# Layer 0 of a four-layer image network on one Trainium2 core: another way to build the position biases, the softmax denominators and the order of the score tiles

## The chip, the core and the metric

One core of one Trainium2 chip runs the whole network in a single launch. The time of a run is the device time in microseconds (us) of that core. A measurement is the median of three runs; a profile is one further execution that the hardware profiler recorded.

The engines are named as the profile names them: PE is the matrix engine, PEld its weight loads, DVE the vector engine, ACT the scalar engine, POOL the GpSimd engine, SP the engine that here only issues DMAs. An entry such as SPq or POOLq is the instruction queue of that engine.

## The reference, cut to what matters

The input `x` is 2 images of 64 by 64 positions with 128 channels. Four layers follow one another; only layer 0 is changed. It adds to `x` a self-attention over the 4096 positions of each image, 4 heads of 32 dimensions, with a bias that depends on the relative row and the relative column of the two positions:

```
qkv = einsum('bhwc,cd->bhwd', _gn(x), w_qkv);  q, k, v = split(qkv)      # _gn: group normalization
rw[q, k] = q . pos_emb_w[column(k) - column(q) + 63]
rh[q, k] = q . pos_emb_h[row(k) - row(q) + 63]
scores = einsum('bnqd,bnkd->bnqk', q, k) / sqrt(32) + rw + rh
attn = softmax(scores, axis=-1)
x = x + einsum('bnqk,bnkd->bnqd', attn, v)
```

(The two bias lines are the reference's `relative_position_bias` with its padding and reshaping written out as an index.) The other layers, a triangle product, two attentions and two expert stages, come after it and are the same in both kernels.

## The kernel before, in words

`layer0` (line 273) works in four **units**, one for each image b and pair of heads p. For a unit it needs the rows of q and k, and for each query the biases against the 64 rows and the 64 columns. Scores with biases are made by one matmul with a contraction of 64: 32 rows of k, then 32 rows that hold a one-hot pattern (in `ka`, lines 300 to 319), against 32 rows of q, 16 rows of row biases and 16 rows of column biases (in `mv`). The one-hot rows pick the two biases that belong to a key.

**Preparation of a unit.** `tokens(b)` (line 333) transposes the image by PE into `xT`, takes its statistics and normalizes it in one DVE instruction (line 353). `project(b)` (line 356) makes v, k (`pk`, line 384) and q (`pq`, line 390) from it; k and q go to DRAM scratch `kd` and `qd` by SP DMAs and q also back into `xT`. `biases(b, p)` (line 400) makes the biases with small matmuls: for each of 64 columns one [64 x 128] by [64 x 64] product with a shifted window of a table `tab` (line 411), and the same for each of 64 rows (line 426). Eight of them fill a PSUM bank, ACT copies it out (lines 419 and 434), and SP writes it to the DRAM scratch `wd` (line 421, one DMA) and `hd` (line 435, eight DMAs). These products have the right diagonal already, because each of the 64 takes its own window of the table.

**Main loop** (line 574). A unit has 8 blocks of 512 queries (`qb`), a block has 4 steps over key rows (`xb`), a step has 8 score tiles (4 `yb` times 2 `s`). A score tile `sc` is [128 keys x 2 heads x 512 queries], made by 4 matmuls that use the four 64 x 64 quarters of the array (line 598). ACT takes the exponential into an `es` tile (line 612; ring of 8), DVE adds it to `acc` (line 620), and PE multiplies it by v into `o` (line 552, four column groups of 32). The order on PE is written out: four score tiles, then the `o` products of four tiles that are two pairs behind (`while len(waiting) > 2`), then one **piece** of side work. A piece is one step of a generator in `side`: the preparation of the next unit, cut at its `yield`s. The first tile of a block is written by ACT into `acc` itself and added to in place.

`mv` has two copies; `prefill(at + 2)` (line 622) queues on SP the loads of the step after next. SP thus carries these loads and all scratch writes, in order.

**Block end.** `finish` (line 502) copies `o` out, and on PE makes 4 products with `fold` (line 513) and 8 products of a [128 x 128] piece of `acc` with a column of ones (line 518), which give the denominators per query. DVE then copies, inverts, multiplies and adds to `x` (lines 527 to 539).

Before the main loop, preparation of unit 0 runs alone (lines 475 to 483). POOL and DVE each build one of the two one-hot tables at the very start (line 305).

Of the kernel before, what the change touches and what calls it, by code (L numbers as in the profile page):

```python
# [38 lines left out]
class Net:  # L39
# [56 lines left out]
    def rstd_parts(self, out, var, eps, n):  # L96

        nc = self.nc
        v = self.small.tile([P, n], F32, tag=f"rs_v{n}", name="rs_v")
        nc.vector.tensor_scalar(v, var, eps, None, ALU.add)  # L100
        s = self.small.tile([P, n], F32, tag=f"rs_s{n}", name="rs_s")
        nc.scalar.activation(s, v, AF.Sqrt)
        yield
        r = self.small.tile([P, n], F32, tag=f"rs_r{n}", name="rs_r")
        nc.vector.reciprocal(r, s)
        q = self.small.tile([P, n], F32, tag=f"rs_q{n}", name="rs_q")
        nc.vector.scalar_tensor_tensor(q, r, -0.5, r, ALU.mult, ALU.mult)
        nc.vector.tensor_tensor(q, q, v, ALU.mult)
        nc.vector.scalar_tensor_tensor(out, q, 1.5, r, ALU.add, ALU.mult)

    def group_stats(self, ps, b, xT=None):
# [3 lines left out]
        st = self.small.tile([P, NC // 4, 6], F32, tag="gst", name=f"gst{b}")  # L115
# [145 lines left out]
    def l0_tables(self, ps, pool, raw, tab):  # L261

        nc = self.nc
        nc.vector.memset(tab, 0.0)
        for i, n in enumerate("hw"):
            pt = ps.tile([P, 512], F32, tag="misc", name=f"l0pe{n}")
            nc.tensor.transpose(pt[:HD, :P], raw[:, i, :], self.ident)
            for h in range(NH):
                nc.scalar.copy(
                    tab[h * HD : (h + 1) * HD, i, : 2 * S - 1, h % 2], pt[:HD, : 2 * S - 1]  # L270
                )

    def layer0(self):
# [4 lines left out]
        pairs = 2  # L278
        with ExitStack() as st:
            wp = st.enter_context(tc.tile_pool(name="l0w", bufs=1))  # L280
            ap = st.enter_context(tc.tile_pool(name="l0b", bufs=2))
            dp = st.enter_context(
                tc.tile_pool(name="l0d", bufs=1, space=bass.MemoryType.DRAM)
            )
            w = self.load(wp, "wqkv", [P, 3 * C], ins["L0_conv_w_qkv"])
            raw = wp.tile([P, 2, HD], F32, tag="raw", name="l0raw")
            nc.vector.memset(raw, 0.0)
            for i, n in enumerate("hw"):
                nc.sync.dma_start(out=raw[: 2 * S - 1, i, :], in_=ins[f"L0_conv_pos_emb_{n}"])
            tab = wp.tile([P, 2, P, 2], F32, tag="tab", name="l0tab")  # L290
            ones = wp.tile([P, 1], F32, tag="ones", name="l0ones")
            nc.vector.memset(ones, 1.0)
            sums = wp.tile([P, 2 * pairs * 8, 4, 2], F32, tag="sums", name="l0sums")

# [5 lines left out]
            kas = []  # L300
            for i in range(2):
                ka = wp.tile([P, L], F32, tag=f"ka{i}", name=f"ka{i}")
                for lo in (32, 96):
                    for g in range(NX):
                        (nc.gpsimd, nc.vector)[i].tensor_tensor(
                            ka[lo : lo + 32, g * TB * S : (g + 1) * TB * S].rearrange(
                                "p (a x y) -> p a x y", x=TB, y=TB
                            ),
                            self.ident[lo : lo + 32, lo : lo + TB]
                            .unsqueeze(1)  # L310
                            .unsqueeze(3)
                            .broadcast_to([32, NX, TB, TB]),
                            self.ident[lo : lo + 32, lo + TB : lo + 32]
                            .unsqueeze(1)
                            .unsqueeze(1)
                            .broadcast_to([32, NX, TB, TB]),
                            ALU.add,
                        )
                kas.append(ka)

            qd = [dp.tile([P, L], F32, tag=f"qd{b}", name=f"l0qd{b}") for b in range(B)]
            kd = [dp.tile([P, L], F32, tag=f"kd{b}", name=f"l0kd{b}") for b in range(B)]
            units = [(b, pair) for b in range(B) for pair in range(pairs)]
            hd = {u: dp.tile([P, L], F32, tag=f"hd{u}", name=f"l0hd{u[0]}_{u[1]}") for u in units}
            wd = {u: dp.tile([P, L], F32, tag=f"wd{u}", name=f"l0wd{u[0]}_{u[1]}") for u in units}
# [6 lines left out]

            def tokens(ps, b):
# [3 lines left out]
                st = self.small.tile([P, NC // 4, 6], F32, tag="gst", name=f"gst{b}")  # L337
# [15 lines left out]
                nc.vector.tensor_scalar(xT, xT, gm, gr, ALU.subtract, ALU.mult)  # L353
                yield

            def project(ps, b):
# [8 lines left out]
                for n in range(NC // 4):  # L365
                    pv = ps.tile([P, 4, C], F32, tag="misc", name=f"l0pv{b}_{n}")
                    for i in range(4):
                        j = 4 * n + i
                        nc.tensor.matmul(
                            pv[:, i, :],  # L370
                            lhsT=xT[:, j * P : (j + 1) * P],
                            rhs=w[:, 2 * C :],
                            start=True,
                            stop=True,
                        )
                    for p in range(pairs):
                        nc.scalar.copy(
                            v[p][:, 4 * n : 4 * n + 4, :], pv[:, :, 2 * HD * p : 2 * HD * (p + 1)]
                        )
                    yield  # L380
                for g in range(L // 512):
                    part = blocks(xT, g)
                    pk = ps.tile([P, NX, P], F32, tag="misc", name=f"l0pk{b}_{g}")
                    nc.tensor.matmul(pk, lhsT=w[:, C : 2 * C], rhs=part, start=True, stop=True)
                    kst = ap.tile([P, NX, P], F32, tag="stage", name=f"l0kst{b}_{g}", bufs=3)
                    nc.scalar.activation(kst, pk, AF.Copy, scale=root)
                    nc.sync.dma_start(out=blocks(kd[b], g), in_=kst)
                    yield
                    pq = ps.tile([P, NX, P], F32, tag="misc", name=f"l0pq{b}_{g}")
                    nc.tensor.matmul(pq, lhsT=w[:, :C], rhs=part, start=True, stop=True)  # L390
                    qst = ap.tile([P, 512], F32, tag="stage", name=f"l0qst{b}_{g}", bufs=3)
                    nc.scalar.copy(
                        qst.rearrange("p (x a y) -> p a x y", a=NX, y=TB),
                        pq.rearrange("p a (x y) -> p a x y", y=TB),
                    )
                    nc.sync.dma_start(out=qd[b][:, g * 512 : (g + 1) * 512], in_=qst)
                    nc.scalar.copy(part, pq)
                    yield

            def biases(ps, b, p):  # L400

                grid = qTs[b].rearrange("p (x a r y) -> p x r a y", x=NX, a=NX, y=TB)
                flat = tab.rearrange("p n i h -> p n (i h)")
                rows = slice(2 * HD * p, 2 * HD * (p + 1))
                t = f"{b}_{p}"
# [1513 lines left out]
```

## Time and profile before

| | |
|---|---|
| median of three runs | 5018.42 us (5015.92 to 5019.35) |
| the profiled execution: its own time | 5015.46 us |
| the profiled execution: span from first to last instruction | 5013.6 us |
| mean granted PE clock | 0.907 |
| first score matmul of layer 0 | 142.5 us |
| last addition of layer 0 to `x` | 1830.3 us |
| block-to-block distance in unit 3, from one copy of `o` to the next | 46.86 us or 48.55 us; mean 47.81 us of seven |
| busy in layer 0 until 1835 us: PE | 1769 us |

The page of a profile has numbered parts: busy time by engine, the span in 40 slices, DMA queues, the chain of work that ended last, and the costliest groups of instructions by line with their mean duration and the idle time before them. Beside the page the trace answers questions: a timeline of a stretch, the windows view (busy time, granted clock and DMA share in given stretches), one line's instructions with their shortest, median and longest duration, and groups with their shapes kept apart. Fp32 matmuls appear as two records each, and four that use different parts of the array overlap, so busy time divided by records gives the spacing.

### The profile page before, as it was taken

How to read it: one execution, taken by the hardware profiler on the slowest of the kernel's cores; microseconds unless marked ns; L12 is line 12 of the kernel's file. 1: busy time of each engine (PE TensorE's matmuls, PEld its weight loads, DVE VectorE, ACT ScalarE, POOL GpSimd, SP SyncE). 2: the span in 40 equal slices, each digit the busy share in tenths (PEclk: the TensorE clock that was granted, in tenths of full speed). 3: DMA queues.
4: the chain of work that ended last, by engine and by line, in shares of the span. 5: the costliest groups of instructions: out<-in, count | busy, mean ns of one | idle time of the engine just before them, and what ended most of it. 6: DMA issues, size and time to landing. Idle time of an engine off the chain costs nothing.

```text
span 5013.6 us, 69136 instructions
## 1 busy us (share of the span) xinstructions
PE 4518.9 (90%) x28099; PEld 2029.4 (40%) x28099; DVE 2904.6 (58%) x4826; ACT 2372.4 (47%) x2781; POOL 681.6 (14%) x450
## 2 busy tenths in 40 slices
PE   7999999999999967468999999967999999999765
PEld 6433333443333325422233233326975444444432
DVE  2567867666878788745666655562042333333577
ACT  3556666565666643235777788841012222222200
POOL 1000000000000011114455455520011000000000
PEclk7899999999999988679999999975569999999889
DMA  4323333333233310000000000021400000000000
GB/s 126 67 56 53 54 68 72 73 82 66 48 62 54 55 29 1 6 19 1 1 1 1 1 1 1 1 70 67 118 19 1 0 0 0 0 0 0 5 13 22
DMA packets 132797, 164.95 MB, mean 33 GB/s; under 512 B 13904, under 2 KB 76208, under 8 KB 131568
## 3 DMA queue, kind: packets, MB, share of 16 engines
q1 hardware_dynamic: 110560, 143.25, 13.4%
q10 hardware_dynamic: 21904, 17.12, 1.2%
q8 instruction: 225, 3.69, 0.3%
q14 instruction: 108, 0.88, 0.1%
HBM read 130.97 MB, written 29.36 MB: 32 GB/s over the span
## 4 chain that ended last, share of the span: by engine, by line
PE 80%; DVE 12%; ACT 5%; issue 1%; DMA 1%; POOL 0%; SPq 0%; DVEq 0%; ACTq 0%; POOLq 0%
PE l0sc L598 18%; PE l0o L552 9%; PE scl L1683 9%; PE oTl L1700 9%; PE l2sc L1312 5%; PE l2pos L1213 4%; PE l2av L1364 4%; PE f3ex L1857 2%; PE f2po L1561 2%; PE f2ph L1535 2%; DVE l0acc L620 2%; PE l0pw L411 2%; ACT l2es L1350 2%; PE l0ph L426 1%; DVE x L1865 1%
## 5 line engine op out<-in xcount | busy, mean ns | idle before, releaser
L620 DVE TENSOR_TENSOR l0acc<-l0acc,l0es 128x1024 f32<-128x1024 f32 x988 | 1210.0, 1225 | 540.1 <-PE l0o L552 376.5
L612 ACT ACTIVATE l0es<-l0sc 128x1024 f32<-128x1024 f32 x992 | 940.3, 1031 | 387.1 <-PE l0sc L598 386.2
L598 PE MATMUL l0sc<-l0mv,ka 64*64 64x512 f32 x8192 | 993.3, 617 | 18.8 <-ACT l0es L612 16.5
L1708 DVE TENSOR_TENSOR accl<-accl,esl 128x1024 f32<-128x1024 f32 x240 | 294.1, 1225 | 540.7 <-ACT esl L1694 482.9
L1339 POOL TENSOR_TENSOR l2es<-l2es 128x1024 f32<-128x1024 f32 (+3 forms) x288 | 505.0, 1753 | 604.4 <-DVE l2es L1336 530.9
L598 PEld LDWEIGHTS l0sc<-l0mv,ka 64*64 64x64 f32 x8192 | 297.8, 136 | 624.3 <-issue 378.4
L1350 ACT ACTIVATE l2es<-l2es 128x1024 f32<-128x1024 f32 (+3 forms) x576 | 533.3, 977 | 6.9 <-POOL l2es L1343 6.7
L1694 ACT ACTIVATE esl<-scl 128x1024 f32<-128x1024 f32 x240 | 245.5, 1023 | 550.8 <-PE scl L1683 550.8
L552 PE MATMUL l0o<-l0es,l0v 128*32 128x512 f32 x3968 | 494.9, 602 | 0.0
L1683 PE MATMUL scl<-l3qT,l3kT 128*128 128x512 f32 x1024 | 484.1, 595 | 1.8 <-DVE bok_l L252 1.8
L1336 DVE TENSOR_SCALAR l2es<-l2sc 128x1024 f32<-128x1024 f32 (+3 forms) x272 | 306.5, 1127 | 296.4 <-PE l2sc L1312 293.7
L1700 PE MATMUL oTl<-esl,l3v 128*128 128x512 f32 x960 | 448.5, 592 | 0.0
L1326 ACT ACTIVATE l2es<-l2sc 128x1024 f32<-128x1024 f32 (+3 forms) x288 | 273.4, 949 | 261.5 <-PE l2sc L1312 258.4
L1312 PE MATMUL l2sc<-l2q,l2kT 32*128 32x512 f32 (+3 forms) x2304 | 339.4, 623 | 10.1 <-DVE l2es L1336 5.8
L1364 PE MATMUL l2av<-l2es,l2v 128*32 128x512 f32 (+3 forms) x2304 | 322.1, 580 | 8.6 <-ACT l2es L1350 8.5
L1213 PE MATMUL l2pos<-l2v,toe 128*32 128x512 f32 (+3 forms) x2304 | 299.9, 582 | 1.4 <-ACT l2v L1158 1.4
L1683 PEld LDWEIGHTS scl<-l3qT,l3kT 128*128 128x128 f32 x1024 | 192.7, 191 | 233.3 <-issue 218.7
L1700 PEld LDWEIGHTS oTl<-esl,l3v 128*128 128x128 f32 x960 | 182.4, 190 | 229.6 <-issue 225.8
L874 POOL TENSOR_TENSOR l1y<-l1y,l1gb 128x1024 f32<-128x1024 f32 x8 | 20.3, 2532 | 1860.6 <-DMA bo<-in_L_conv_bo_dram 1821.6
L552 PEld LDWEIGHTS l0o<-l0es,l0v 128*32 128x32 f32 x3968 | 106.9, 109 | 337.8 <-issue 337.8
L1312 PEld LDWEIGHTS l2sc<-l2q,l2kT 32*128 32x128 f32 x2304 | 100.6, 188 | 255.3 <-ACT l2es L1350 94.3
L1865 DVE SCALAR_TENSOR_TENSOR x<-f3ex,f3wt,x 128x128 f32<-128x128 f32 x512 | 160.2, 347 | 28.5 <-PE f3ex L1857 20.0
(438 smaller groups left out, 4310.8 us busy)
## 6 DMA issues: line engine op xcount, KB each, us to landing
l0mv<-l0qd SPq DMA_DIRECT2D x128, 256.0 KB, 7.6
l0mv<-l0hd SPq DMA_DIRECT2D x256, 128.0 KB, 7.5
l0mv<-l0wd SPq DMA_DIRECT2D x128, 128.0 KB, 5.6
l0wd<-l0rw SPq DMA_DIRECT2D x4, 2048.0 KB, 6.8
l0hd<-l0hst SPq DMA_DIRECT2D x32, 256.0 KB, 2.1
f2w<-in_L_ffn_weight_dram ACTq DMA_DIRECT2D x32, 256.0 KB, 11.9
f2w<-in_L_ffn_weight_dram ACTq DMA_DIRECT2D x8, 1024.0 KB, 5.1
f2w<-in_L_ffn_weight_dram SPq DMA_DIRECT2D x8, 1024.0 KB
```

The lines of the kernel that those rows point to most:

```text
L552: nc.tensor.matmul(o[0][at : at + HD, :], lhsT=v[:, 2 * j + s, HD * h : HD * (h + 1)], rhs=es[s][:, h, :], start=(j == 0), stop=(j == NX * ...
L598: nc.tensor.matmul(sc[64 * c : 64 * c + 64, h, :], lhsT=ka[rows, k0 : k0 + 64], rhs=mv[rows, yb, :], start=True, stop=True,)
L612: nc.scalar.activation(es, sc, AF.Exp)
L620: nc.vector.tensor_tensor(entry[5], entry[5], es, ALU.add)
L1213: nc.tensor.matmul(pos[c : c + 32, j0:, :], lhsT=toe[:, d * P + c : d * P + c + 32], rhs=v[:, n0 + j0 - d : n0 + 4 - d, :], start=(d == n0 ...
L1312: nc.tensor.matmul(sc[:, h2, off:], lhsT=kT[hs, cols], rhs=q[hs, off:], start=True, stop=True,)
L1336: nc.vector.tensor_scalar(es[:, :, lo:], sc[:, :, lo:], root, None, ALU.mult)
L1339: nc.gpsimd.tensor_tensor(part, part, part, ALU.mult)
L1350: nc.scalar.activation(e[:, :, off:], e[:, :, off:], AF.Silu)
L1364: nc.tensor.matmul(avs[i][hs, off:], lhsT=vs[b][:, k, hs], rhs=es[h // 2][:, h % 2, off:], start=(k == 0), stop=last,)
L1683: nc.tensor.matmul(sc[:, i, :], lhsT=kT[:, k * P : (k + 1) * P], rhs=qs, start=True, stop=True,)
L1700: nc.tensor.matmul(oT, lhsT=v[:, k, :], rhs=es[:, i, :], start=(k == 0), stop=(k == NC - 1),)
```

## The change

All of it is in layer 0 and its helpers.

1. **Full-width bias products.** `slope` multiplies all 127 rows of the (flipped) position table, as a [32 x 128] weight for one head, by 512 queries at once, two heads into one [128 x 2 x 512] PSUM tile. This holds the products of every query with every relative offset. It is copied out as one [128 x 1024] tile in the `es` ring and written to new DRAM scratch (`slopes`). The right diagonal is then picked by the addresses of a DMA: `skewed` reads with a row step of L and a step of L + S from one group to the next, in runs of 64 numbers. For the row biases the DMA goes from scratch to `hd`; for the column biases into a tile `tw`, which POOL copies, reordered, into `rw`; four DMAs write `rw` to `wd`. The row order in `hd` and `wd` is reversed, and the one-hot tables and the `mv` indices follow that.
2. **Queues.** Every DMA of `project` and `biases` is issued by POOL, no longer by SP. The table loads are issued by ACT, each row four times over (one copy for each head).
3. **One-hot tables on POOL.** Both are built there from a small reversed identity, after the tokens of image 0.
4. **Denominators.** `block_end` multiplies a [128 x 32] tile of ones by `acc` in four column groups, 512 queries wide, so that `zb` has the layout of `o`. ACT copies it out (with a running sum for the range check), DVE inverts 128 x 512 numbers and multiplies `os`, and the `fold` products come last; DVE adds their PSUM result to `x` directly.
5. **Rounds of eight.** A step makes its 8 score tiles, then its 16 pairs of `o` products; there is no `waiting` list. `acc` has its own tile, written first as `es[0,0] + es[0,1]`. The `es` ring is 9. One piece of side work per step, two in the last step of a block and in all steps of unit 1.
6. Small things: `tokens` normalizes in 4 parts, `project` goes by 4 groups of rows, for unit 0 some copies go to DVE, small tiles have fewer buffers.

The order in which the compiled kernel's instructions stand on the engines follows the program: on PE eight score tiles, eight tiles' `o` products, a slope. On POOL stand, ahead of the first DMA of `project`, all 16 one-hot instructions; then for each unit 32 writes of slopes, 16 skewed reads into `tw` with 8 copies between them, 16 skewed scratch-to-scratch copies into `hd` and 4 writes of `wd`.

The diff, cut to its core:

```diff
+            def skewed(t, first, rows, n):
+                at = t[:, :]
+                return bass.AP(
+                    tensor=at.tensor,
+                    offset=at.offset + first * (L + S),
+                    ap=[[L, rows], [L + S, n], [1, S]],
+                )
...
-                    nc.sync.dma_start(out=blocks(kd[b], g), in_=kst)
+                        nc.gpsimd.dma_start(out=blocks(kd[b], g), in_=kst)
...
+            def slope(ps, u, n, g, tag):
+                pt = ps.tile([P, 2, 512], F32, tag="sc", name=f"l0p{t}", bufs=tag[1])
+                for h in range(2):
+                    rows = slice((2 * p + h) * HD, (2 * p + h + 1) * HD)
...
+                    nc.tensor.matmul(
+                        pt[:, h, :],
+                        lhsT=pos[rows, "hw".index(n), :],
+                        rhs=rhs,
...
+                ev = ap.tile([P, 2, 512], F32, tag=tag[0], name=f"l0e{t}", bufs=tag[2])
...
+                for h in range(2):
+                    nc.gpsimd.dma_start(
+                        out=slopes[h, n][u][:, g * 512 : (g + 1) * 512], in_=ev[:, h, :]
+                    )
+            def biases(ps, u, tag):
...
+                def turned(g):
+                    tw = ap.tile([P, 8, S], F32, tag="tw", name=f"l0tw{b}_{p}_{g}", bufs=1)
+                    for h in range(2):
+                        nc.gpsimd.dma_start(
+                            out=tw[S * h : S * h + S],
+                            in_=skewed(slopes[h, "w"][u], 8 * g, S, 8),
+                        )
+                    nc.gpsimd.tensor_copy(
+                        rw.rearrange("p (x y) -> p y x", y=S)[:, 8 * g : 8 * g + 8, :], tw
+                    )
+                for g in range(8):
+                    slope(ps, u, "w", g, tag)
+                    if g >= 2:
+                        turned(g - 2)
+                    yield
+                for g in range(8):
+                    slope(ps, u, "h", g, tag)
...
+                    for h in range(2):
+                        nc.gpsimd.dma_start(
+                            out=hd[u][S * h : S * h + S, g * 512 : (g + 1) * 512].rearrange(
+                                "k (x y) -> k x y", y=S
+                            ),
+                            in_=skewed(slopes[h, "h"][u], 8 * g, S, 8),
+                        )
+                    yield
...
+                zb = ps.tile([P, 512], F32, tag="misc", name=f"l0zb{t}")
+                for s in range(2):
+                    for h in range(2):
+                        at = 64 * s + HD * h
+                        nc.tensor.matmul(
+                            zb[at : at + HD, :],
+                            lhsT=ones,
+                            rhs=acc[:, h, :],
...
+                r = ap.tile([P, 512], F32, tag="zs", name=f"l0zs{t}", bufs=1)
+                nc.scalar.activation(r, zb, AF.Copy, accum_out=sums[:, 0, n : n + 1])
+                yield
+                nc.vector.reciprocal(r, r)
+                nc.vector.tensor_tensor(os, os, r, ALU.mult)
...
+                if i == 1 or xb == 3:
                     piece()
+                piece()
                 prefill(at + 2)
```

## The prediction, as put on record

> **What bounds the kernel now.** I read the page's chain of waits first, then its groups, the windows view for the start, and the timeline of a steady stretch. The change touches only layer 0, the first 1830 us of a span of 5013.6 us (the execution took 5015.46 us, 3 us under the median of 5018.42).
>
> ```profile
> PE 80%; DVE 12%; ACT 5%; issue 1%; DMA 1%; POOL 0%; SPq 0%; DVEq 0%; ACTq 0%; POOLq 0%
> L620 DVE TENSOR_TENSOR l0acc<-l0acc,l0es 128x1024 f32<-128x1024 f32 x988 | 1210.0, 1225 | 540.1 <-PE l0o L552 376.5
> L598 PE MATMUL l0sc<-l0mv,ka 64*64 64x512 f32 x8192 | 993.3, 617 | 18.8 <-ACT l0es L612 16.5
> ```
>
> PE carries 80% of the chain, and the score matmuls were held for 18.8 us in all. DVE waits 540 us, so it is not the bound; but 376 of these are one wait per block: the first addition into `acc` waits until PE has read that tile as a value operand, and DVE then runs behind.
>
> ```profile
> 1512.85 3.66 PE L598 MATMUL l0sc<-l0mv,ka 64*64 64x512 f32 x32
> ...
> 1514.01 3.77 ACT L612 ACTIVATE l0es<-l0sc 128x1024 f32<-128x1024 f32 x4 [1.79 <-PE l0sc L598]
> ...
> 1516.45 1.92 PE L552 MATMUL l0o<-l0es,l0v 128*32 128x512 f32 x16
> ...
> 1518.30 3.66 PE L598 MATMUL l0sc<-l0mv,ka 64*64 64x512 f32 x32
> ```
>
> That is one PE cycle, four score tiles and four tiles' values: 5.45 us from 1512.85 to 1518.30. It holds 12 groups of four overlapping records. In the same timeline the weight loads of a group start every 0.43 us, so the work is 12 x 0.43 = 5.16 and the two switches cost 0.29. ACT needs 0.94 per tile against 1.36 of PE.
>
> ```profile
> 36.00:66.00 30.00, 22.39 (x97) 0.90 0.52 160
> 66.00:93.00 27.00, 27.00 (x127) 0.50 0.22 57
> 93.00:121.00 28.00, 27.75 (x131) 0.50 0.39 150
> 121.00:142.00 21.00, 16.08 (x71) 0.50 0.39 75
> ```
>
> This is the start (length, PE busy, records, granted clock, DMA share, GB/s). From 66 to 121 us PE does nothing but the narrow bias products of unit 0, at a granted clock of 0.50: 0.21 us a record, against 0.127 later (6.09 us for 48 records). The first score matmul comes at 142.5.
>
> **The main loop, 142.5 to 1830 us.** A clean block takes 46.86 us (from one copy of `o` to the next in unit 3); every other one takes 48.55, because PE runs a cycle at half speed (5.36 us instead of 3.66, roughly every 50 to 100 us). The mean is 47.81. I keep these 0.95 us per block.
>
> - *Rounds of eight:* 24 groups x 0.43 = 10.32, and one pair of switches, 0.29, instead of two. 10.61 a round, 42.4 a block, against 43.6: -1.2.
> - *Denominators:* the block end takes 2.9 us of PE now (24 records from 1502.94 to 1505.71 and a switch). It gets 4 `zb` products that overlap on four column groups like the values, 2 x 0.43 = 0.86, and 8 `fold` records at 2.77/24 = 0.115, 0.92, each with a switch of 0.1: 2.0 in all, -0.9.
> - *Own `acc` tile:* the remaining 0.3 us of a clean block is a hold of the score matmuls behind ACT, where DVE has not freed `es`. It goes, as DVE no longer waits 7 us per block.
>
> PE then needs 44.5 + 0.95 = 45.4 us a block. **DVE is next:** back to back, 19 additions took 25.14 us, 1.32 each, so 31 cost 40.9. New is an inversion of 128 x 512:
>
> ```profile
> L529 DVE RECIPROCAL l0ri<-l0sums 128x8 f32<-128x8 f32 x32 | 6.3, 195 | 0.0
> L1829 DVE RECIPROCAL f3ri<-f3ri 128x64 f32<-128x64 f32 x1 | 0.6, 550 | 0.0
> ```
>
> 355 ns for 56 more columns is 6.3 ns a column, so 3.4 us for 512 (an estimate from these two rows). With the product (0.69, the row of 128x512) and the addition to `x` (0.42) DVE has 45.7 us a block. That is PE's time within 1%: where no side work runs, about half of the blocks, I take 46.0. So 32 blocks cost 16 x 45.4 + 16 x 46.0 = 1462 instead of 32 x 47.81 = 1530: **-68**.
>
> - *Bias products of units 1 to 3:* lines 411 and 426 keep PE busy for 92 us after 142. Instead there are 48 slopes. Their two heads lie on different rows of the array; if they overlap, a slope is 2 x 0.43 and a switch, 0.96, if not 1.82; 46 or 87 us. The products of line 1312, also 32 rows deep, overlap (339.4 us for 2304 records, 0.147 each), so I take 46: **-46**. The first score tiles of before also came at a clock of 0.66, and pieces are fewer but larger, fewer switches: **-15**.
>
> Together the loop gains about 130 us, if nothing new holds it.
>
> **The new queue.** POOL has no DMA in the trace of before; after the change it issues, for each unit, 32 slope writes, 32 skewed copies and 4 writes of `wd`, and does 8 copies of 128x512 (1.26 us by line 968). Call the cost of one issue t. From below SP's own issues bound it: 0.34 us for `hd`, 0.38 for `kd` with four times the runs. From above I take POOL's nearest compute row:
>
> ```profile
> L305 POOL TENSOR_TENSOR ka<-ident x8: 1913/2852/2910, 1.4 to 18.5; 32x1024 f32<-32x1024 f32 x8
> L305 DVE TENSOR_TENSOR ka<-ident x8: 1214/2897/2949, 5.3 to 23.5; 32x1024 f32<-32x1024 f32 x8
> ```
>
> up to 2.9 us (1.9 while DVE is not beside it). I choose t = 1.0, nearer to SP's rows, since these are the same operation. A landing takes 2.1 to 2.3 us (writes to scratch).
>
> *Start:* 16 one-hot instructions at 1.91 keep POOL until 33 us; DVE, freed of its eight, no longer delays the statistics (they start at 24.8 now, when DVE is done), so tokens are ready by then. `project` waits for 16 issues and 4 copies and some landings: 33 + 16t + 5 + 8 = 62. The first scores need `wd`, and on POOL's queue 52 issues and 8 copies stand before it is written: 52t + 10 = 62, so 124; one landing and the `mv` load (5.6 by its row) make 132. That is -10. At t = 0.35, with landings that no longer hide, about 104 (-38); at t = 2.9, 261 (+118). PE runs ahead, but the nine `es` slots hold its slopes until POOL has written them.
>
> *In the loop:* a piece costs POOL 4t + about 1. While unit 0 runs there are 5 pieces in a block of 46 us, one per 9.2 us: fine until t = 2. In unit 1 two come per round of about 12: fine until t = 1.25. Beyond it the slope's `es` slot comes free late, ACT cannot write the next `es`, and the score matmuls stand behind ACT. At t = 1: +8 (the double piece in the last step). At t = 2.9: 16 pieces at 12.2 are 196 us against 147, 96 and 147 on hand: +198.
>
> POOL's copies lie beside DVE's additions; in the pair of lines above a DVE row of 1.21 became 2.9 beside POOL. 28 copies could cost DVE up to 1.7 us each, 48 us, but they fall in blocks with side work, where PE has 2 to 4 us to spare. I take 0.
>
> Sum at t = 1: -130 - 10 + 8 = -132 on 5018: **4886**.
>
> [...]
>
> **Rivals.**
>
> - *A, forecast:* t below about 1.5; POOL keeps up. 4850 to 4930. For it: POOL is idle in layer 0 after 21 us, DMA share is 0.32.
> - *B: the queue is felt but not decisive,* t of 1.5 to 2: the start ends at 160 to 195 and unit 1 waits. With t = 1.8: start +44, unit 1 +37, loop -130: 4970.
> - *C: slower; POOL's queue is the bound of preparation.* Its price is 68 us of start per us of t, and the stalls above; it decides from about t = 2.1. At 2.9 it gives 118 + 198 - 130 = +186, 5204. For it: 68 issues a unit where SP made 9, half of them of 512 runs of 256 B; against it: SP's rows hardly grow with the runs, and the transfers themselves are no bound (`kd`, 512 runs of 512 B, lands in 2.3 us).
> - *D: not what it says.* Eight tiles in a row make ACT late (0.94 against PE's 0.86 a tile), and DVE, not PE, sets the block, with POOL's copies at their full price: 47 us a block and 48 us more. Loop -50 instead of -130: 4966.
>
> **Chances.** A 0.55, B 0.12, C 0.27, D 0.06. The range goes from 4840 (t = 0.35: -38 - 130 = -168, 4850, and a little) to 5150 (t = 2.6), which leaves out a few in a hundred below and about a third of C above, and takes in B, D and the slopes that do not overlap (+41). A's own range is 4840 to 4940. Faster by over 0.2% (about 10 us, what a measurement here can tell from no change) holds for A, D and most of B: 0.68; within 0.2%: 0.05; slower: 0.27.
>
> **What would show it.** The first score matmul near 132 us (C: after 200). POOL's DMA issues near 1 us. Blocks of unit 3 at 46 us, with a round every 10.6. Slope records at 0.43 a pair. DVE's wait for `o` gone from its line, and the inversion at 3.4 us. It is wrong if ACT's exponentials wait for DMA landings in units 0 to 2 (C), or if score matmuls in unit 3 wait for ACT and ACT for DVE (D).

## The result and the profile after

The changed kernel takes 5070.64 us (5068.9 to 5077.37), the kernel before 5017.17 us on the same chip: a ratio of 1.0115, 95% interval 1.0095 to 1.0135. It is **slower** by 1.2%. The profiled execution has a span of 5070.3 us.

First, where. The first transposition of the next layer's normalized input (tile `l1pt`) starts at 1854.0 us in the trace of before and at 1908.6 after: 54.6 us, all but 2 us of the difference of the two spans, lie before this mark. It stands 24 us behind layer 0's last addition to `x` in both. I call it "end of layer 0" from here on and compare the experiments by it: a later stage that no edit touches (from the start of the last `l2sc` matmul to the start of the first `f2ph` matmul) takes 141.0 us in before's trace, 145.8 after and 129 to 146 in the experiments, which blurs whole times.

Then, what. From the page after the change, the chain of waits and the two costliest groups (busy us, mean ns | idle before, releaser):

```profile
PE 60%; issue 16%; DVE 15%; ACT 5%; DMA 3%; POOL 1%; DVEq 0%; SPq 0%; ACTq 0%; POOLq 0%
L688 DVE TENSOR_TENSOR l0acc<-l0acc,l0es 128x1024 f32<-128x1024 f32 x960 | 1184.9, 1234 | 269.1 <-ACT l0es L683 176.7
L675 PE MATMUL l0sc<-l0mv,ka 64*64 64x512 f32 x8192 | 1012.6, 633 | 146.6 <-ACT l0es L683 79.2
```

PE fell from 80% of the chain to 60%. DVE's big wait for PE's `o` products, 376 us before, is gone as forecast. But PE's score matmuls now wait 146.6 us where they waited 18.8: 79.2 of these for ACT. So: what does ACT wait for? The waits view, from 142 us on (us in total, times, longest):

```profile
ACT l0zs L626 <- DVE l0os L625: 202.5, 31, 8.4
```

One instruction, once per block. Line 626 is the small ACT instruction that sums the inverted denominators for the range check. The timeline of a block of unit 3 shows what stands behind it. DVE, ACT and PE in turn:

```profile
1520.11 7.88 DVE L688 TENSOR_TENSOR l0acc<-l0acc,l0es 128x1024 f32<-128x1024 f32 x6
1527.90 3.35 DVE L624 RECIPROCAL l0zs<-l0zs 128x512 f32<-128x512 f32 x1
1531.28 0.69 DVE L625 TENSOR_TENSOR l0os<-l0os,l0zs 128x512 f32<-128x512 f32 x1
```

```profile
1524.05 0.69 ACT L622 ACTIVATE l0zs<-l0zb 128x512 f32<-128x512 f32 x1
...
1532.01 0.63 ACT L626 ACTIVATE l0zs<-l0zs 128x512 f32<-128x512 f32 x1 [7.19 <-DVE l0os L625]
...
1532.64 2.83 ACT L683 ACTIVATE l0es<-l0sc 128x1024 f32<-128x1024 f32 x3
```

```profile
1523.56 3.62 PE L697 MATMUL l0o<-l0es,l0v 128*32 128x512 f32 x32
1527.11 2.81 PE L675 MATMUL l0sc<-l0mv,ka 64*64 64x512 f32 x24
1533.69 7.41 PE L675 MATMUL l0sc<-l0mv,ka 64*64 64x512 f32 x40 [3.78 <-ACT l0es L683]
1541.03 3.64 PE L697 MATMUL l0o<-l0es,l0v 128*32 128x512 f32 x32
```

The denominators are in ACT's tile at 1524.7, but DVE comes to them only at 1527.9, after the additions queued ahead, and is done at 1532.0. ACT waits 7.19 us for it with the next step's exponentials behind. PE fills the three score tiles that the kernel keeps in PSUM (24 records) and stops: 3.78 us. When it goes on, its 40 records take 7.41 us; at the full rate, 64 records in 7.10 us, they would take 4.4. The windows view of the same stretch gives the reason (length, PE busy, PEld, DVE, ACT, POOL busy, granted clock, DMA share, GB/s):

```profile
1533.69:1539.65 5.96, 5.96 (x30) 1.76 (x34) 5.54 (x5) 4.25 (x5) 0.00 (x0) 0.51 0.00 0
1539.65:1543.00 3.35, 3.35 (x36) 0.96 (x32) 3.04 (x4) 2.53 (x3) 0.00 (x0) 1.00 0.19 59
```

For 6 us after the pause PE has half its clock: 3 us more. Pause and half rate make the 51.2 us of a block of unit 3, every block, against 46.86 or 48.55 before.

### The profile page after: what moved, and what is told of

Read it like the earlier page. It is cut to its first block, busy times and chain, and to the rows that moved or that the text cites. A ratio compares the mean times of both kernels' runs of the same rounds, so it can differ in the third digit from the quotient of the medians.

```text
span 5070.3 us, 67659 instructions
## 1 busy us (share of the span) xinstructions
PE 4445.1 (88%) x27079; PEld 1880.8 (37%) x27079; DVE 3023.0 (60%) x4811; ACT 2394.0 (47%) x2871; POOL 929.2 (18%) x809
## 4 chain that ended last, share of the span: by engine, by line
PE 60%; issue 16%; DVE 15%; ACT 5%; DMA 3%; POOL 1%; DVEq 0%; SPq 0%; ACTq 0%; POOLq 0%
PE scl L1770 9%; PE oTl L1787 9%; PE l0sc L675 8%; PE l2sc L1399 5%; PE l2pos L1300 4%; PE l2av L1451 4%; DVE l0acc L688 4%; PE l0o L697 3%; PE f3ex L1944 2%; PE f2po L1648 2%; PE f2ph L1622 2%; ACT l2es L1437 2%; DVE l0zs L624 1%; DVE x L1952 1%; DMA l0tw<-l0sw 1%
## 5 line engine op out<-in xcount | busy, mean ns | idle before, releaser
L688 DVE TENSOR_TENSOR l0acc<-l0acc,l0es 128x1024 f32<-128x1024 f32 x960 | 1184.9, 1234 | 269.1 <-ACT l0es L683 176.7
L675 PE MATMUL l0sc<-l0mv,ka 64*64 64x512 f32 x8192 | 1012.6, 633 | 146.6 <-ACT l0es L683 79.2
L683 ACT ACTIVATE l0es<-l0sc 128x1024 f32<-128x1024 f32 x1024 | 962.5, 1048 | 213.0 <-PE l0sc L675 195.4
L675 PEld LDWEIGHTS l0sc<-l0mv,ka 64*64 64x64 f32 x8192 | 313.0, 140 | 820.0 <-issue 370.5
L697 PE MATMUL l0o<-l0es,l0v 128*32 128x512 f32 x4096 | 468.6, 594 | 2.1 <-ACT l0es L683 2.1
L1399 PE MATMUL l2sc<-l2q,l2kT 32*128 32x512 f32 (+3 forms) x2304 | 340.4, 624 | 10.1 <-DVE l2es L1423 5.9
L697 PEld LDWEIGHTS l0o<-l0es,l0v 128*32 128x32 f32 x4096 | 123.6, 110 | 332.1 <-issue 326.9
L1944 PE MATMUL f3ex<-ew,f3xnT 128*128 128x512 f32 x256 | 125.8, 613 | 55.1 <-DVE x L1952 55.1
```

Source lines behind the costliest of these rows:

```text
L675: nc.tensor.matmul(sc[64 * c : 64 * c + 64, h, :], lhsT=ka[rows, k0 : k0 + 64], rhs=mv[rows, NX - 1 - yb, :], start=True, stop=True,)
L683: nc.scalar.activation(es[yb, s], sc, AF.Exp)
L688: nc.vector.tensor_tensor(acc, acc, es[yb, s], ALU.add)
L697: nc.tensor.matmul(o[lo : lo + HD, :], lhsT=v[:, 2 * (xb * NX + yb) + s, HD * h : HD * (h + 1)], rhs=es[yb, s][:, h, :], start=(xb == 0 an ...
L1399: nc.tensor.matmul(sc[:, h2, off:], lhsT=kT[hs, cols], rhs=q[hs, off:], start=True, stop=True,)
```

## The experiments

Theory 1: the check's place on ACT's queue costs, and nothing else does as much. Theory 2: DVE sets the block, and ACT's wait only shows it. Blocks are distances between copies of `o` in unit 3. The kernel before ran beside each group of runs, at medians of 5017 to 5022 us.

| run | median us | first scores | end of layer 0 | block, us |
|---|---|---|---|---|
| before | 5017.17 | 142.5 | 1854.0 | 46.86 / 48.55 |
| changed | 5070.64 | 139.8 | 1908.6 | 51.20 |
| late_check | 5075.69 | 140.2 | 1913.2 | 51.20 |
| no_check (one run) | 4923.49 | 141.4 | 1765.2 | 44.29, then 44.95 |
| held_check | 4942.4 | 141.1 | 1772.4 | 44.29, then 44.95 |
| short_inversion (one run) | 4941.75 | 140.6 | 1777.1 | 45.43 |
| half_inversion (one run) | 5003.76 | 141.6 | 1840.3 | 46.97 / 48.45 |
| narrow_denominators | 4955.42 | 142.8 | 1799.5 | 45.16 / 46.86 |
| straight_w (one run) | 5060.6 | 139.8 | 1897.2 | 51.20 |
| gathered_w (one run) | 4938.97 | 139.4 | 1774.3 | 44.29, then 44.95 |
| both_fixes | 4915.32 | 131.6 | 1752.5 | 44.95 / 45.30 |
| two_tw | 4906.82 | 131.4 | 1747.0 | 44.95 / 45.30 |
| pool_columns | 4898.93 | 132.8 | 1732.4 | 44.95 / 45.30 |
| one_piece | 4926.95 | 132.2 | 1760.1 | 44.95 / 45.30 |

**late_check.** The check moves one `yield` down in the program.

```diff
                 nc.vector.tensor_tensor(os, os, r, ALU.mult)
-                nc.scalar.activation(r, r, AF.Copy, accum_out=sums[:, 1, n : n + 1])
                 yield
+                nc.scalar.activation(r, r, AF.Copy, accum_out=sums[:, 1, n : n + 1])
```

> Only the place of one ACT instruction changes: the check of the inverted denominators (line 626) is issued one step later, just ahead of the fold products, when the inversion is long done. Theory 1 (this instruction stands on ACT's queue ahead of the next step's exponentials and waits for DVE): the 6.9 us that a block of unit 3 loses after it (3.8 us idle PE and 3.1 us at half rate) go, blocks of unit 3 fall from 51.2 to 45-46 us, ACT's wait for DVE at this line falls from 202 us to under 10, and the time from 5070 to 4870-4910. Theory 2 (DVE sets the block: 31 additions at 1.32, inversion, product and two more instructions, and ACT's wait only shows it): the same lateness comes back as exponentials that wait for a free es slot; blocks stay at 49-51 us and the time at 5030-5075. Theory 3 (eight tiles in a row make ACT late on their own): as theory 2 in time, but the waits lie at every round, not once a block.

Nothing moved: the time is 1.0108 (1.0091 to 1.0125) of that before, and the wait is there unchanged (waits view, the line is now 627):

```profile
ACT l0zs L627 <- DVE l0os L625: 203.1, 31, 8.4
```

This looks like theory 2, but it is no test. The compiled order has the check at the same place as before, between the copy of `zb` and the first exponential of the next step: the tool that orders the instructions put it back; why is not known. Only the source had changed. Its result says nothing for or against either theory.

**no_check.** The check is left out; the second range check reads the plain denominators.

```diff
-                nc.scalar.activation(r, r, AF.Copy, accum_out=sums[:, 1, n : n + 1])
...
-            self.within(sums[:, 1, :], 0.0, 1e20)
+            self.within(sums[:, 0, :], 0.0, 1e20)
```

> The check of the inverted denominators is left out (the second range check reads the plain denominators again). Theory 1: same as the late check within its own 0.6 us of ACT per block, so within 20 us of it, 4860-4900. Theory 2: 5030-5070. If it is more than 30 us under the late check, the instruction costs something where it is moved to as well.

4923.49 us and blocks of 44.29: theory 2 (blocks of 49 to 51) is out. The time missed the expected 4860-4900, because blocks with side work stayed long (below). Blocks of units 2 and 3 are 44.29 us as long as DVE can fall behind, then 44.95, when DVE's timeline has no gap left: the prediction had this bound at 45.7.

**held_check.** The check stays, and its place is forced behind the next step's exponentials (an edge that orders the queue, without a wait).

```diff
-                nc.scalar.activation(r, r, AF.Copy, accum_out=sums[:, 1, n : n + 1])
                 yield
+                with tc.issue_after(last[0].ins):  # the step's last exponential
+                    nc.scalar.activation(r, r, AF.Copy, accum_out=sums[:, 1, n : n + 1])
```

> The same move as in the late check, but now the order on ACT's queue is forced: the check of the inverted denominators is queued behind the eighth exponential of the following step, one step later than in the changed kernel. Nothing else changes. Theory 1 (only its place on the queue costs, because it waits there for DVE with the exponentials behind it): its wait for DVE falls from 203 us to under 5, blocks of unit 3 are 44.3-45.0 us as without the check, time 4918-4935. Rival (the instruction costs by its own duration on ACT, 0.82 us a block, because ACT is nearly the bound): 4945-4955. Rival 2 (the wait comes back at another instruction): over 5000.

0.9839 (0.9822 to 0.9856) against before. The end of layer 0 comes 136.2 us earlier than in the changed kernel, with the same instructions in another order on one queue. ACT's timeline in unit 3: the check now follows the eight exponentials without any wait.

```profile
1474.34 7.44 ACT L684 ACTIVATE l0es<-l0sc 128x1024 f32<-128x1024 f32 x8 [3.77 <-PE l0sc L676]
1481.84 0.63 ACT L628 ACTIVATE l0zs<-l0zs 128x512 f32<-128x512 f32 x1
```

Against no_check layer 0 is 7.2 us longer, in blocks of units 0 and 1, where the check now stands ahead of copies of slopes (six of them wait 25 us for it). The median is 7 us over the expected range and 3 under that of the first rival (the check costs by its own duration); the untouched later stage took 145.9 us in this profile, 135.7 in that of no_check. The blocks decide between the two: 44.29 us as without the check, where the rival would make each 0.8 longer. Theory 1 holds: the check's place is the cause of the loss.

**short_inversion, half_inversion.** How much wait makes how much loss? The inversion covers 8 or 256 of 512 columns; the other denominators stay uninverted.

```diff
-                nc.vector.reciprocal(r, r)
+                nc.vector.reciprocal(r[:, :8], r[:, :8])      # 256 in half_inversion
```

> The inversion covers 8 of 512 columns (the rest of the denominators stays uninverted, so the output is another), the check stays where it is. Theory 1: ACT waits 7.2 us a block, of which 3.15 is the inversion and about 4 are DVE's backlog of additions; PE's idle stretch of 3.8 us shrinks to about 0.6 us, and with so short a pause the half-rate stretch goes too: blocks of unit 3 at 45.5-47.5 us, time 4900-4960. Theory 2 (DVE sets the block): blocks fall by the inversion alone, 3.15 us, to 48.0, time 4960-4975, and the half-rate stretch stays.

> The inversion covers 256 of 512 columns (the other half of the denominators stays uninverted, so the output is another), the check stays at its early place. The wait of ACT is then 1.48 us longer than with 8 columns (1.67 against 0.19 us). Theory A (PE loses only the pause itself, and the half rate after it comes from elsewhere): blocks of unit 3 at 45.43 + 1.48 = 46.9 us, 4985. Theory B (a pause of about 2 us is enough to set PE to half rate for about 6 us): 46.9 + 3.1 = 50.0 us, 5050-5060. Theory C (the half-rate stretch grows with the pause): on the line between 45.43 (8 columns) and 51.19 (512 columns), 48.1 us, about 5005.

With 8 columns the block is a steady 45.43 us (theory 1) and PE's pause 0.69, with no half rate:

```profile
1532.29 4.75 PE L675 MATMUL l0sc<-l0mv,ka 64*64 64x512 f32 x40 [0.69 <-ACT l0es L683]
```

With 256 the time and the mean of seven blocks, 47.8 us, lie near theory C, but no single block does: they go between A's 46.9 and 48.45, nearly in turn. Two successive blocks of half_inversion, first line of each the three score tiles ahead of the pause:

```profile
1532.57 2.81 PE L675 MATMUL l0sc<-l0mv,ka 64*64 64x512 f32 x24
1537.61 4.75 PE L675 MATMUL l0sc<-l0mv,ka 64*64 64x512 f32 x40 [2.23 <-ACT l0es L683]
...
1579.55 2.81 PE L675 MATMUL l0sc<-l0mv,ka 64*64 64x512 f32 x24
1584.58 6.22 PE L675 MATMUL l0sc<-l0mv,ka 64*64 64x512 f32 x40 [2.23 <-ACT l0es L683]
```

and their granted clock (windows view, third number from the end):

```profile
1537.60:1540.60 3.00, 2.99 (x28) 0.83 (x32) 2.79 (x3) 3.00 (x4) 0.00 (x0) 1.00 0.00 0
1584.58:1587.60 3.02, 3.02 (x16) 0.93 (x20) 2.81 (x3) 2.76 (x3) 0.00 (x0) 0.56 0.00 0
```

The same pause of 2.23 us is followed by full rate once and by half rate the next time, for about 3 us, so the blocks go between 46.97 and 48.45. The pause of 3.78 brings half rate in every block of unit 3, for 6 us, that of 0.69 never.

The trace's own record of the granted clock says more. In unit 3 its half-rate stretches last 6.83 us in the changed kernel and 3.41 in half_inversion, two steps and one of the same length, and they begin on a grid of such steps: in the traces of before and of the changed kernel all 51 and 61 half-rate stretches begin on one grid of 3.413 us, to 0.003 us. In half_inversion one begins at 1584.94. The pause before it (1582.36 to 1584.58) lies whole in the step that ends there. The pause of the block before (1535.38 to 1537.61) is cut by the grid, at 1537.15, into 1.77 and 0.46 us, and no half rate follows. Laid on the grid in this way, the ten pauses of half_inversion and the eleven of the changed kernel from 1250 us on part cleanly: where one step holds 2.00 us of a pause or more, half rate follows; where none holds more than 1.93, it does not. The changed kernel's block of 51.20 us is 15 steps, so its pauses in unit 3 all fall alike, about 2.8 us in one step and 0.9 in the next, and the half rate lasts for two.

**narrow_denominators.** Rounds of eight, own `acc` and slopes stay; the block end is that of the kernel before (no long inversion, no second check; the range check covers half of the denominators).

```diff
-                zb = ps.tile([P, 512], F32, tag="misc", name=f"l0zb{t}")
+                po = ps.tile([P, 4, P], F32, tag="misc", name=f"l0po{t}")
+                for i in range(4):  # fold products into po[:, i, :64]
+                    for h in range(2):
+                        nc.tensor.matmul(po[:, i, at : at + 1], lhsT=acc[:, h, cols], rhs=ones[:, :1], ...)
```

> The changed kernel with the block end of the kernel before: 4 fold products and 8 products of a piece of acc with a column of ones, one DVE copy, a small inversion, a multiplication, an addition; no inversion of 512 columns and no second ACT check (the range check covers half of the denominators). Rounds of eight, the own acc tile and the new slopes stay. If only the check's place made the change slower, this block end is as good as any: PE needs 44.29 - 2.16 + 2.9 = 45.0 us a block. Theory N (the 24 narrow records of this block end are what sends PE to half speed for a cycle, in every second block as in the kernel before): unit 3 alternates between 45.0 and 46.7 us. Rival (the half speed of before came from the holds of score matmuls behind ACT and DVE): a steady 45.0. Time 4935-4965 by N, 4925-4940 by the rival; with DVE freed of 3.3 us a block, blocks with side work may gain some us against the run without the check (4923).

0.9877 (0.9856 to 0.9898) against before. Blocks are 45.16 or 46.86, mostly in turn: theory N. PE's timeline, the last of the narrow records and the step after them, in two blocks:

```profile
1552.63 0.56 PE L619 MATMUL l0po<-l0ones,l0acc 128*128 128x1 f32 x4
1553.12 7.10 PE L676 MATMUL l0sc<-l0mv,ka 64*64 64x512 f32 x64
...
1597.80 0.56 PE L619 MATMUL l0po<-l0ones,l0acc 128*128 128x1 f32 x4
1598.29 8.79 PE L676 MATMUL l0sc<-l0mv,ka 64*64 64x512 f32 x64
```

The granted clock at the start of the second step (windows view):

```profile
1598.63:1602.04 3.41, 3.41 (x20) 1.07 (x16) 1.97 (x4) 1.33 (x2) 0.00 (x0) 0.50 0.00 0
```

PE is never idle here, yet the second step takes 1.69 us more: 2.8 us of records only 1 or 64 columns wide are enough for 3.41 us of half clock. On the grid of steps through 1598.63 the narrow records ahead of it (from 1595.52) lie whole in one step, those of the block before (from 1550.35) are cut at 1550.84. From 1250 us on, in this run and in the kernel before, half rate follows where one step holds 2.49 us of them or more, and not where it holds 2.38 or less. The prediction kept 0.95 us a block for a half-speed cycle "roughly every 50 to 100 us" as if it belonged to the chip; it belonged to this block end, and without it unit 3 shows no half clock: in no_check the granted clock is 1.00 from 1450 to 1700 us, in held_check from 1460 to 1700. The full-width denominators are worth 27 to 34 us of layer 0 (1799.5 against 1765.2 without and 1772.4 with the held check), once their check does not stand in the way.

**straight_w, gathered_w.** The column slopes read every 64th number of `q`. straight_w reads neighbouring ones (so the column biases belong to other queries); gathered_w, on top of the held check, lets ACT copy them together first.

```diff
-                        rhs = q.rearrange("p (x y) -> p y x", y=S)[:, 8 * g : 8 * g + 8, :]
+                        rhs = q[:, g * 512 : (g + 1) * 512]    # straight_w
+                        rhs = qc[rows]                         # gathered_w: qc copied by ACT
```

> The 32 slopes of the column biases read their 512 queries from neighbouring columns, not every 64th (so the column biases belong to other queries, and the output is another). If the step of 64 numbers halves the rate of the moving operand, their two records go from 1.96 us a slope to the 1.13 us of the row slopes: 32 x 0.83 = 27 us of PE less, 20 of them after 142 us; where PE is the bound in units 0 to 2 the time falls by 15 to 25 us, to 5045-5055. If PE is not the bound there (ACT's late check sets those blocks as well), it falls by under 8 us.

> On top of the held check: for each slope of the column biases ACT first copies its 512 queries into a tile with neighbouring columns (32 copies more of 64 partitions by 512 numbers, about 0.6 us each), and PE reads that tile. If the step of 64 numbers of the moving operand is what doubled PE's time, these slopes fall from 1.96 to about 1.13 us, 32 x 0.83 = 27 us, 20 of them after the start, and the time is 15 to 25 us under the held check. Rival (the copies stand ahead of exponentials on ACT and cost what PE gains): within 8 us of it.

The groups of the column slopes after 142 us, in the changed kernel and in straight_w:

```profile
L485 PE MATMUL l0pw<-l0xT,l0pos 32*128 32x512 f32 x96 | 45.7, 1056 | 0.0
L485 PE MATMUL l0ph<-l0xT,l0pos 32*128 32x512 f32 x96 | 24.9, 622 | 0.0
```

```profile
L485 PE MATMUL l0pw<-l0xT,l0pos 32*128 32x512 f32 x96 | 27.2, 666 | 0.0
```

Contiguous operands save 18.5 us of PE; layer 0 ends 11.4 us earlier and the run is 10 us shorter, between the two expectations (15 to 25, or under 8). In gathered_w PE saves as much, but the copies take ACT 1.10 us each, and the end of layer 0 is 1.9 us later than with the held check: the rival. Part of this is another wait: the long block between units 1 and 2 goes from 66.95 to 73.22 us, so one run here does not separate it from the copies. both_fixes and two_tw below, where that block is nearly alike, do. The prediction had put no price on the step of 64 numbers, and only steps of 64 and of 1 were run.

**both_fixes, two_tw.** A second buffer for `tw`, with and without the gathering (the small statistics tiles go back to two buffers, for room).

```diff
-                    tw = ap.tile([P, 8, S], F32, tag="tw", name=f"l0tw{b}_{p}_{g}", bufs=1)
+                    tw = ap.tile([P, 8, S], F32, tag="tw", name=f"l0tw{b}_{p}_{g}", bufs=2)
```

> On top of the gathered slopes: two buffers for the tile tw that the skewed DMAs fill, so that POOL's copy of one and the landing of the next overlap (and the small statistics tiles have two buffers again, as before, to make room). If POOL's chain of issues, landings and copies sets the start, 8 landings of which 0.6 to 1.8 us were waited for (8.9 us together) overlap, the first score matmul comes at 128-134 us instead of 141, and the time is 7 to 13 us under the gathered slopes; the total is then about 4890-4905, 2.3% under the kernel before. Rival (the start is bound by the number of issues and copies alone): no change within 4 us.

> The held check and two buffers for tw, without the gathered slopes (the small statistics tiles have two buffers, to make room). From the pair before it: the second buffer brought the first score matmul from 139.4 to 131.6 us, and the long block between units 1 and 2 from 73.2 to 54.3 us. Without the gathered copies this should hold: first scores at 132-133 us, layer 0 done 15 to 22 us earlier than with the held check alone, 4910-4925. If the gathering on ACT gained anything, this is slower than both fixes (4915) by over 5 us; if it cost something, faster.

PE's first score matmul, in the changed kernel and in two_tw:

```profile
139.77 11.76 PE L675 MATMUL l0sc<-l0mv,ka 64*64 64x512 f32 x64 [41.56 <-DMA l0mv<-l0wd]
```

```profile
131.42 5.77 PE L676 MATMUL l0sc<-l0mv,ka 64*64 64x512 f32 x24 [34.32 <-DMA l0mv<-l0wd]
```

Against held_check the first scores come ten us earlier (141.1 to 131.4), and the long block between units 1 and 2 falls from 66.95 us to 55.35. So POOL's chain of issue, landing and copy through one buffer was a bound, in the start and in unit 1. two_tw is at 0.978 (0.9761 to 0.9799), both_fixes at 0.9799 (0.9786 to 0.9812); without the gathering layer 0 is 5.5 us shorter.

**pool_columns.** POOL gathers, one slope ahead, in units 1 to 3.

```diff
+                copy = nc.scalar.copy if tag[3] else nc.gpsimd.tensor_copy
+                qc = columns(u, 0, copy)
                 for g in range(8):
+                    slope(ps, u, "w", g, tag, qc)
+                    if g < 7:
+                        qc = columns(u, g + 1, copy)
```

> Both fixes, but in units 1 to 3 POOL, not ACT, copies the queries for the column slopes into neighbouring columns, one slope ahead (24 copies of 64 x 512). Theory (the gathering on ACT gave back what PE gained, as ACT stands 0.94 us a tile against PE's 0.86 in a step): with ACT free of them PE keeps its 0.83 us a slope, 24 x 0.83 = 20 us less than with two buffers of tw alone, about 4895. Rival (DVE is slowed by POOL's copies beside it, or POOL's queue delays the slopes): no gain against two buffers alone, 4910-4925.

Layer 0 ends 14.6 us before that of two_tw, of the 20 expected. In whole time, 0.9775 (0.9754 to 0.9796), its five runs spread from 4875 to 4913 (in the profiled one, 4875, the untouched later stage took 129 us, in two_tw's 145) and the intervals of the two overlap; that it is the faster one is shown only for layer 0 of the profiled runs. POOL's copy takes 1.42 us in the mean beside DVE. Both beat the kernel before by 2.2%.

**one_piece.** Of two_tw, unit 1 with one piece of side work per step.

```diff
-                if i == 1 or xb == 3:
+                if xb == 3:
```

> The kernel with the held check and two tw buffers, with one piece of side work per step in unit 1 too (two only in the last step of a block, as in the other units); its 40 pieces then just fill the unit. Theory (two pieces in a step cost more than their products: in unit 1 of the run before it a step took 58.3/4 = 14.6 us against 11.1 without pieces, 1.75 a piece, where a piece's products take 1.13, because a few score records stand alone between them): the same pieces cost about 1.2 each, so 30 x 0.6 = 18 us less in unit 1; against that unit 2's biases are ready only in the last step, and its first score waits 10 to 20 us for POOL's copies and DMAs and the mv load. Sum within 10 us of 4907. Rival (a piece costs 1.75 wherever it stands): unit 1 as long as before, and the wait comes on top: 4915-4930.

4926.95, 0.9807 (0.979 to 0.9825): the rival. Unit 1's blocks with five pieces take 55.2 us, with eight 58.3, so a piece costs more alone (2.2 us) than paired (1.75). In the kernel before a `project` piece made a cycle about 1.1 us longer. What two_tw adds shows on PE:

```profile
644.77 1.16 PE L429 MATMUL l0pv<-wqkv,l0xT 128*128 128x128 f32 x8
645.85 1.07 PE L676 MATMUL l0sc<-l0mv,ka 64*64 64x512 f32 x2
646.85 1.16 PE L429 MATMUL l0pv<-wqkv,l0xT 128*128 128x128 f32 x8
647.94 7.09 PE L676 MATMUL l0sc<-l0mv,ka 64*64 64x512 f32 x62
```

Two score records stand alone between two pieces and take 1.07 us, while the 62 that are left take as long as 64: about 1 us for each of 12 steps. In one_piece five pieces of unit 1 wait for DVE's addition of `po` to `x`, which frees the PSUM buffer they share (tag `misc`), 13 us in all (4 in two_tw), and from 540 to 960 us the mean granted clock is 0.96 against 0.98; unit 2 also starts later. More than that about its side work the runs do not settle.

## Why the prediction was wrong

The forecast was 4886, faster; the change is slower. Step by step:

- **What failed: the denominators' term.** It priced 4 + 8 products at -0.9 us a block and DVE's inversion, and said of the own `acc` tile that DVE "no longer waits 7 us per block". It never listed line 626, an ACT instruction that the diff adds and that waits for DVE, and so never asked what is queued behind it on ACT. That wait, 6.5 us a block, took the place of DVE's, and on ACT the exponentials stand behind it; PE's pause and the half rate after it follow. It costs 136.2 us (changed against held_check). Without it the sign of the forecast is right: 0.9839 instead of 1.0115.
- **"What would show it" had the sign, rival D the wrong cause.** D let score matmuls wait for ACT and ACT for DVE, but for the eight tiles in a row, at 47 us a block. Eight tiles in a row do no harm: blocks of 44.29 with the check held.
- *Rounds of eight:* forecast 10.61 us, measured 10.60. *Denominators on PE:* 2.0 forecast, 1.9 measured from start to start (0.88 and 1.03; 4 x 10.60 + 1.9 gives the block of 44.3). *Inversion:* 3.4 forecast, 3.35 measured. *DVE's 45.7 us a block:* 44.95; the four terms named add up to 45.4. These sizes hold. (Rival D's loop is -40 by its own terms, not -50.)
- *Clean blocks:* better than forecast, 44.29 to 44.95 instead of 45.4 to 46.0, since the half-speed cycle, kept at 0.95, came with the narrow records. Over the 32 blocks, 24 x (47.81 - 44.29) + 8 x (47.81 - 44.85) = 108 us, not 68.
- *Side work and slopes:* forecast -46, -15 and +8, -53 in all. Held_check's layer 0 is 81.6 us shorter than before's; less the 108 and 1.4 of start, the side work costs 28 us **more** than before, 81 us away from the forecast. Of these 81 the slopes are 25 (70.6 us after 142 instead of 46, the strided operand), the 15 that I granted for the clock of 0.66 and fewer switches and that nothing shows, about 12 the lone score records, 7 the held check. Some 20 are left; the long block between units 1 and 2, from which the second `tw` buffer took 11.6, is probably among them, the rest is open.
- *POOL's issue:* t = 1.0 was too dear. Slope writes take 0.55 in the start and 0.56 later, skewed copies 0.70:

```profile
L498 POOL DMA_DIRECT2D l0sw<-l0ew x16 | 8.7, 550 | 4.7 <-ACT l0ew L496 3.8 <-DVE l0ew L494 0.9
...
L498 POOL DMA_DIRECT2D l0sw<-l0ew x48 | 26.6, 558 | 236.7 <-ACT l0ew L496 234.5 <-issue 2.1
```

  The 48 beside DVE's additions are as quick (558 ns) as the 16 without them (550 ns). So C was not what happened.
- *Start:* forecast 132 at t = 1, measured 139.8, near only by luck. At 0.6 the same sum would have given 33 + 16 x 0.6 + 13 = 56, then 52 x 0.6 + 10 = 41 and 8, so 105: the issues were too dear and the waits missing. On POOL's timeline `project` ends at 70.4, not 56: POOL waits 20.5 us for ACT's copies of k, 10.1 of them for the first, since ACT is still at the tokens' statistics at 35.8, when POOL has been free from 33 on. From there to the last write of `wd`, at 131.1, it takes 60.7, not 41: POOL waits 4.8 us for the first slopes to land, 9.1 for the eight `tw` before it copies them, 1.4 for `hd` and 4.7 for the engines that fill the slopes. The landings of `biases`' DMAs take 3.0 to 6.6 us by the page after, not 2.1 to 2.3. The one buffer for `tw` is worth 8 to 10 us of the start, as two_tw shows.

## What to carry to other kernels

Go through a diff by engine queue, not by purpose: for each added instruction, however small, write down what it waits for and what stands behind it; a check of 0.6 us cost 136 because it stood ahead of the exponentials. Look up the compiled order before you believe that a line moved in the source has moved on the queue, and force it where it matters. When a pause or a stretch of narrow matmuls recurs in every block, price the slow clock that may follow it as well: here 3 us after a pause of 3.78, and 1.5 to 1.7 in about every second block after one of 2.23 or after 2.8 us of narrow records.

## What was not expected of the hardware

- In unit 3 PE's granted clock falls to half after a pause of 3.78 us in every block, after 2.23 us in about every second, after 0.69 in none; and in about every second after 2.8 us of 1- and 64-column records without any pause. Laid on the grid of 3.41 us steps, the cases seen from 1250 us on part by how much of them falls into one step: 2.00 us of pause or more against 1.93 or less, 2.49 us of narrow records or more against 2.38 or less.
- A moving operand read with a step of 64 numbers makes two heads' slope take 1.96 us instead of 1.13 on PE, and read in a row (straight_w) the 24 slopes after 142 us take 27.2 us instead of 45.7; the same gathering takes ACT 1.10 us for 64 x 512 numbers, against 0.59 for its copies of 128 x 512.
- 960 additions on DVE went from 1.225 to 1.234 us in the mean with POOL's copies and DMAs beside them: about 9 us in all, not the 48 that I had set as the worst case.
